# Batch norm's scale in the last stage: from ScalarE alone to GpSimd and ScalarE by turns

## The chip, the cores and the metric

The kernel runs on one core of a Trainium2 chip. The metric is the device time of one execution in microseconds. Before the change it is 2118.17 us, the median of six runs (2117.89 to 2119.62). The core has five engines that matter here: TensorE (PE) multiplies matrices, VectorE (DVE), ScalarE (ACT) and GpSimd (POOL) work elementwise, and SyncE (SP) issues DMA transfers. Each works through its own queue in order and waits on semaphores for the others.

## The reference

Sixteen images x of 128 channels and 32x32 pixels, in f32, pass through an attention layer and a residual block of two quantized convolutions. What matters here is the end of the second:

```python
out = act_quant(x)
out = conv3x3(out, weight_quant(w1))
out = batchnorm(out, gamma1, beta1)
out = act_quant(out)
out = conv3x3(out, weight_quant(w2))
out = batchnorm(out, gamma2, beta2)
return out + identity
```

`batchnorm` takes mean and variance of each channel over all sixteen images, so no image can be scaled before the last one's second convolution is done. With the statistics known it is `y * scale + bias` with one scale and one bias per channel; then the block's input (`identity`) is added.

## The kernel before

Channels lie on the 128 partitions, so an image is a tile of 128x1024 f32 (512 KB). `fast_path` runs in two parts. The first, the attention of all images and the first convolution, takes nearly all of the span; the attention's result of each image is stored to DRAM (`x1_dram`). The second part (lines 836 to 876) brings these back as `res0` to `res15` (`x1` in the code), computes the first batch norm's parameters, and then goes over the images: `quantize` the image, nine matmuls per piece in `conv` (L273), ScalarE's copy out of PSUM into the image's tile `ys[b]` (L284), VectorE's `bn_stats` (L283, L289). Between them `check_sums` (L337 to L351) works out a flag, with one `partition_all_reduce` on GpSimd (L350); if it is set, a slower general path runs afterwards (L1061, L1062), which is not the case with these inputs.

`bn_params(1)` (L306 to L327) then turns the statistics into `scale2` and `bias2`, in a chain of small VectorE instructions and one of ScalarE. It ends with the bias (L324). Everything before this point is left as it is.

The last stage is lines 866 to 876. It goes over the images in order; some of the first are cut into parts along their pixels. For each part there are three steps: `y * scale2 + bias2` in place, on VectorE for the first two parts of image 0 (L872) and on ScalarE for all else (L874); the addition of the residual in place, on VectorE (L875), with both inputs in SBUF; and the store to `out`, issued by SP (L876).

The order of instructions on each engine is set by the tile framework's scheduler, which takes the program's order with dependencies in mind; each engine then runs its own list in order. A tile's addition waits for its scaling and for its `res` transfer, a store waits for its addition.

GpSimd has sixteen instructions in the whole span: memsets at the start (L222, L231, L236, L296), the identity for transposes (masks.py, lines 197 and 199), two `partition_all_reduce` for the convolution weights (L1042) and the one of L350. [...]

Of the kernel before, what the change touches and what calls it, by code (L numbers as in the profile page):

```python
# [12 lines left out]
ALU = mybir.AluOpType  # L13
# [176 lines left out]
def fast_path(  # L190
# [13 lines left out]
    B, C, N = x.shape  # L204
# [27 lines left out]
    ys = [keep.tile([P, N], F32, name=f"y{b}") for b in range(B)]  # L232
# [6 lines left out]
    def quantize(b, src, scale, bias, r0=0, r1=H):  # L239

        cut = slice(r0 * W, r1 * W)
        t = qtp.tile([P, (r1 - r0) * W], F32, tag="qt", name="qt")
        if b == B - 1 and scale == A_LEVELS and r1 == H:
            nc.vector.tensor_scalar(t, src[:, cut], scale, 0.0, ALU.mult, ALU.max)
        else:
            nc.scalar.activation(t, src[:, cut], AF.Relu, bias=bias, scale=scale)
        nc.vector.tensor_scalar(t, t, A_LEVELS, MAGIC, ALU.min, ALU.add)
        return nc.vector.tensor_scalar(  # L248
            pads[b % NPAD][:, r0 + 1 : r1 + 1, 1 : W + 1],
            t.rearrange("p (h w) -> p h w", w=W),  # L250
            MAGIC,
            None,
            ALU.subtract,
        )
# [7 lines left out]
    def gather(n):  # L262
        nc.vector.bn_aggr(late[n][:, 1:3], early[n].rearrange("p g s -> p (g s)"))
        nc.vector.tensor_scalar(
            late[n][:, 2:3], late[n][:, 2:3], float((B - 1) * N), None, ALU.mult
        )

    def conv(pool, tag, b, n, r, rows=RPH, group=None, after=None):

        ps = pool.tile([P, rows, W], F32, tag=tag, name=f"psc{n}_{b}_{r}")  # L270
        for tap in range(NTAP):
            dy, dx = divmod(tap, 3)
            last = nc.tensor.matmul(  # L273
                ps,
                lhsT=wq[n][:, tap, :],
                rhs=pads[b % NPAD][:, r + dy : r + dy + rows, dx : dx + W],
                start=(tap == 0),
                stop=(tap == NTAP - 1),
            )
        ps = ps.rearrange("p h w -> p (h w)")  # L280
        if group is not None:
            with tc.issue_after(after) if after else nullcontext():
                nc.vector.bn_stats(place(n, b, group), ps)  # L283
        nc.scalar.copy(ys[b][:, r * W : (r + rows) * W], ps)  # L284
        return last

    def statistics(b, n):
        for hf in range(NHF):
            last = nc.vector.bn_stats(place(n, b, hf), ys[b][:, ts(hf, HALF)])  # L289
        return last  # L290
# [15 lines left out]
    def bn_params(n):  # L306

        new = lambda what: keep.tile([P, 1], F32, name=f"{what}{n}")
        mv = keep.tile([P, 2], F32, name=f"mv{n}")
        nc.vector.bn_aggr(mv, late[n])  # L310
        mean, var = mv[:, 0:1], mv[:, 1:2]
        rt = new("rt")
        nc.scalar.activation(rt, var, AF.Sqrt, bias=eps, scale=ss[:, n : n + 1])
        v = new("v")
        nc.vector.tensor_scalar(v, var, ss[:, n : n + 1], BN_EPS, ALU.mult, ALU.add)
        r = new("r")
        nc.vector.reciprocal(r, rt)

        t = new("t")
        nc.vector.tensor_scalar(t, r, r, v, ALU.mult, ALU.mult)  # L320
        nc.vector.tensor_scalar(t, t, -0.5, 1.5, ALU.mult, ALU.add)
        scale, bias = new("scale"), new("bias")
        nc.vector.tensor_scalar(scale, r, t, gs[:, n : n + 1], ALU.mult, ALU.mult)
        nc.vector.scalar_tensor_tensor(  # L324
            bias, mean, scale, be[:, n : n + 1], ALU.mult, ALU.subtract, reverse1=True
        )
        return scale, bias  # L327
# [9 lines left out]
    def check_sums():  # L337

        sums_range(B - 1)
        ok = keep.tile([P, 2], F32, name="ok")  # L340
        low, high = keep.tile([P, 1], F32, name="low"), keep.tile([P, 1], F32, name="high")
        nc.vector.tensor_reduce(low, ext[:, 0, :], AX.X, ALU.min)
        nc.vector.tensor_reduce(high, ext[:, 1, :], AX.X, ALU.max)
        nc.vector.tensor_scalar(ok[:, 0:1], low, 1.0 / SUM_LIMIT, None, ALU.is_ge)
        nc.vector.tensor_scalar(ok[:, 1:2], high, SUM_LIMIT, None, ALU.is_le)
        bad = keep.tile([P, 1], F32, name="bad")
        nc.vector.tensor_tensor(bad, ok[:, 0:1], ok[:, 1:2], ALU.mult)
        nc.vector.tensor_scalar(bad, bad, -1.0, 1.0, ALU.mult, ALU.add)
        worst = keep.tile([P, 1], F32, name="worst")
        nc.gpsimd.partition_all_reduce(worst, bad, P, bass_isa.ReduceOp.max)  # L350
        nc.vector.tensor_copy(flag, worst[0:1, :])  # L351

    with ExitStack() as ph:
# [454 lines left out]
        while step < n_steps or later:  # L808
            if step < n_steps:
                g, j = divmod(step, NCH)  # L810
                b, h = heads[g]
# [24 lines left out]
    with ExitStack() as ph:  # L836
        pool = lambda name, bufs, **kw: ph.enter_context(tc.tile_pool(name=name, bufs=bufs, **kw))
        resp = pool("res", 1)
        ps_c = pool("ps_c", 6, space=PSUM)
        scale1, bias1 = bn_params(0)  # L840
        x1 = []
        for b in range(B):
            t = resp.tile([P, N], F32, name=f"res{b}")
            nc.sync.dma_start(out=t, in_=x1d[b])
            x1.append(t)

        for r0, r1 in ((0, 10), (10, RPH + 2), (RPH + 2, H)):
            quantize(0, ys[0], scale1, bias1, r0, r1)
        quantize(1, ys[1], scale1, bias1)
        starts = {0: (0, 8, RPH, H), B - 1: (0, RPH, H - 8, H)}  # L850
        for b in range(B):
            rows = starts.get(b, (0, RPH, H))
            for i, (r0, r1) in enumerate(zip(rows, rows[1:])):
                conv(ps_c, "c", b, 1, r0, r1 - r0, group=i if b == B - 1 else None)
            if b + 2 < B:
                quantize(b + 2, ys[b + 2], scale1, bias1)
            if b < B - 1:
                done = statistics(b, 1)
            if b == B // 2:
                with tc.issue_after(done.ins):  # L860
                    check_sums()
            if b == B - 2:
                gather(1)
        scale2, bias2 = bn_params(1)

        parts = {0: (0, N // 4, N // 2, N), 1: (0, N // 2, N), 2: (0, N // 2, N)}
        for b in range(B):
            ends = parts.get(b, (0, N))
            for lo, hi in zip(ends, ends[1:]):
                y = ys[b][:, lo:hi]  # L870
                if b == 0 and hi <= N // 2:
                    nc.vector.tensor_scalar(y, y, scale2, bias2, ALU.mult, ALU.add)  # L872
                else:
                    nc.scalar.activation(y, y, AF.Identity, bias=bias2, scale=scale2)  # L874
                nc.vector.tensor_tensor(y, y, x1[b][:, lo:hi], ALU.add)  # L875
                nc.sync.dma_start(out=out[b][:, lo:hi], in_=y)  # L876
    outer.close()
# [107 lines left out]
def attention_then_quantized_convs(  # L985
# [48 lines left out]
    def conv_weights(n, wp, behind):  # L1034
# [19 lines left out]

    flag = const.tile([1, 1], mybir.dt.int32, name="flag")
    fast_path(
        nc, tc, x, wqk, wvo, bo, bnp, x1d, out, bo_sb, bnp_sb, quad, wq, sc, flag, conv_weights,
        constants,
# [81 lines left out]
```

## Time and profile before

| What | Value |
|---|---|
| median of six runs | 2118.17 us |
| the profiled execution, its own time | 2117.95 us |
| its span, from first to last instruction | 2116.1 us |
| PE busy | 2084.5 us (99%) |
| DVE busy | 1454.5 us (69%) |
| ACT busy | 735.9 us (35%) |
| POOL busy | 6.8 us, 16 instructions |
| last bias known (L324) | 2089.56 us |
| L874 on ACT, 128x1024, x13 | 1225 ns each |
| L874 on ACT, 128x512, x5 | 801 ns each |
| L872 on DVE, 128x256, x2 | 408 ns each |
| L875 on DVE, 128x1024, x13 | 1217 ns each |
| L875 on DVE, 128x512, x5 | 680 ns each |
| L875 on DVE, 128x256, x2 | 414 ns each |
| output stores, 512 KB, x13 | 4.1 us from issue to landing (median) |
| output stores, all 20 | 1.7 to 5.4 us from issue to landing |
| stores of `x1_dram`, 512 KB, x16 | 2.6 us from issue to landing (median) |

Times inside the execution are counted from the start of the span. The execution's own time is 1.85 us longer than its span. Consecutive instructions of one engine overlap a little: where VectorE's additions of 1217 ns stand back to back, they start every 1.13 us, those of 680 ns every 0.60 us, those of 256 elements every 0.33 us. The stage that the change touches is the time from 2089.6 us to the end.

### The profile page before, as it was taken

To read this page: it belongs to the slowest core of one execution; us is meant where nothing else is said; L and a number is where in the kernel's file an instruction comes from. 1 tells how busy PE (TensorE), PEld (TensorE's weight loads), DVE (VectorE), ACT (ScalarE), POOL (GpSimd) and SP (SyncE) were. 2 spreads that over 40 slices of the span, in tenths; PEclk is the share of its full clock that TensorE was granted. 3 is DMA by queue.
4 is the path that set the end of the run, shared out by engine and by line. 5 is a ranking of instruction groups with operands and counts; after the bars stand their busy time and mean duration, and the time that the engine had idled before them with its cause. 6 is when DMAs were issued, how large, how long until landed. Compare 5 with 4: busy or idle time off the path is not lost.

```text
span 2116.1 us, 14861 instructions
## 1 busy us (share of the span) xinstructions
PE 2084.5 (99%) x5276; PEld 941.0 (44%) x5277; DVE 1454.5 (69%) x2171; ACT 735.9 (35%) x858; POOL 6.8 (0%) x16
## 2 busy tenths in 40 slices
PE   9999999999999999999999999999999999999994
PEld 4444444444444444444444444444444444444542
DVE  4775677767577676667658666776757667676776
ACT  2333333333333333333333333333333333333365
POOL 0000000000000000000000000000000000000000
PEclk9999999999999999999999999999999999999997
DMA  2000000000000000000000000000000000000044
GB/s 61 12 20 0 0 20 0 20 0 10 11 0 20 0 20 0 1 20 0 20 1 20 0 0 20 0 20 0 13 8 0 20 0 10 0 0 10 1 170 160
DMA packets 11089, 36.81 MB, mean 17 GB/s; under 512 B 1536, under 2 KB 1920, under 8 KB 11008
## 3 DMA queue, kind: packets, MB, share of 16 engines
q1 hardware_dynamic: 9824, 33.10, 4.3%
q10 hardware_dynamic: 1184, 2.69, 0.4%
q8 instruction: 43, 0.70, 0.1%
q14 instruction: 38, 0.31, 0.0%
HBM read 19.01 MB, written 16.78 MB: 17 GB/s over the span
## 4 chain that ended last, share of the span: by engine, by line
PE 98%; DVE 1%; ACT 0%; DMA 0%; issue 0%; ACTq 0%; DVEq 0%
PE pss L487 42%; PE psa L511 41%; PE psv L466 5%; PE psu L453 5%; PE psc L273 3%; PE psw L720 1%; DVE y L875 1%; PE psa L628 1%; ACT y L874 0%; DMA x<-in_x_dram 0%; DVE es L620 0%; PE psr L552 0%; DVEq L1061 0%; DVE late L283 0%; PE ps_b L425 0%
## 5 line engine op out<-in xcount | busy, mean ns | idle before, releaser
L500 ACT ACTIVATE e<-pss 128x1024 f32<-128x1024 f32 x511 | 522.8, 1023 | 1280.4 <-PE pss L487 1244.2
L487 PE MATMUL pss<-u,x 128*128 128x512 f32 (+1 forms) x2064 | 962.4, 589 | 0.0
L511 PE MATMUL psa<-e,vo 128*128 128x512 f32 x2016 | 947.8, 592 | 0.0
L522 DVE TENSOR_TENSOR es<-es,e 128x1024 f32<-128x1024 f32 x378 | 460.5, 1218 | 291.4 <-ACT e L500 291.3
L487 PEld LDWEIGHTS pss<-u,x 128*128 128x128 f32 x2064 | 392.1, 190 | 487.2 <-issue 470.9
L511 PEld LDWEIGHTS psa<-e,vo 128*128 128x128 f32 x2016 | 378.1, 190 | 452.2 <-issue 451.0
L474 DVE COPY vo<-psv 128x512 f32<-128x512 f32 x128 | 88.2, 689 | 265.1 <-PE psv L466 265.1
L453 PE MATMUL psu<-x,at_sb 128*128 128x512 f32 x256 | 131.5, 595 | 0.8 <-DMA x<-in_x_dram 0.5
L466 PE MATMUL psv<-bt_sb,x 128*128 128x512 f32 x256 | 130.2, 592 | 0.0
L534 DVE TRANSPOSE_TENSOR_REDUCE part<-es 128x32 f32<-128x1024 f32 (+1 forms) x66 | 80.6, 1221 | 2.2
L520 DVE TENSOR_TENSOR es<-e,e 128x1024 f32<-128x1024 f32 x63 | 76.6, 1216 | 6.3 <-ACT e L500 6.3
L570 DVE STREAM_TRANSPOSE rb<-sums 128x1024 f32<-128x1024 f32 (+1 forms) x66 | 79.8, 1209 | 1.3
L453 PEld LDWEIGHTS psu<-x,at_sb 128*128 128x128 f32 x256 | 48.7, 191 | 62.3 <-issue 60.3
L466 PEld LDWEIGHTS psv<-bt_sb,x 128*128 128x128 f32 x256 | 48.6, 190 | 61.2 <-issue 57.6
L711 DVE TENSOR_TENSOR tiles<-rows 128x1024 bf16<-128x1024 bf16 x60 | 71.8, 1218 | 1.1 <-PE psw L720 0.6
L458 DVE TENSOR_SCALAR u<-psu,au_sb 128x512 f32<-128x512 f32 x64 | 47.6, 744 | 34.5 <-PE psu L453 34.5
L273 PE MATMUL psc<-pad,wq 128*128 128x512 bf16 (+3 forms) x333 | 67.8, 365 | 0.6 <-DVE pad L248 0.6
L727 ACT COPY wino<-psw 128x512 f32<-128x512 f32 x120 | 64.2, 593 | 0.0
L581 DVE TENSOR_TENSOR av<-av,rb 128x1024 f32<-128x1024 f32 x47 | 57.3, 1220 | 0.4
L582 DVE TENSOR_TENSOR acc<-acc,av 128x1024 f32<-128x1024 f32 x47 | 57.1, 1215 | 0.0
L273 PEld LDWEIGHTS <-wq 128*128 128x128 bf16 x333 | 32.2, 97 | 36.4 <-PE unread L755 1.1
L527 ACT COPY av<-psa 128x512 f32<-128x512 f32 x63 | 36.9, 585 | 29.8 <-PE psa L511 29.8
(121 smaller groups left out, 746.9 us busy)
## 6 DMA issues: line engine op xcount, KB each, us to landing
x_dram<-x SPq DMA_DIRECT2D x16, 512.0 KB, 2.6
res<-x_dram SPq DMA_DIRECT2D x16, 512.0 KB, 9.4
x<-in_x_dram SPq DMA_DIRECT2D x14, 512.0 KB, 3.6
out_dram<-y SPq DMA_DIRECT2D x13, 512.0 KB, 4.1
out_dram<-y SPq DMA_DIRECT2D x5, 256.0 KB, 2.3
raw<-in_cw_dram ACTq DMA_DIRECT2D x2, 576.0 KB, 3.7
x<-in_x_dram ACTq DMA_DIRECT2D x1, 512.0 KB, 3.7
wqk_sb<-in_wqk_dram ACTq DMA_DIRECT2D x1, 385.5 KB, 4.2
```

The source lines that it names most:

```text
L273: last = nc.tensor.matmul(ps, lhsT=wq[n][:, tap, :], rhs=pads[b % NPAD][:, r + dy : r + dy + rows, dx : dx + W], start=(tap == 0), stop=(t ...
L453: nc.tensor.matmul(ps, lhsT=at_sb[:, h, :], rhs=xt[b][:, ts(hf, HALF)], start=True, stop=True)
L466: nc.tensor.matmul(ps, lhsT=xt[b][:, ts(j, P)], rhs=bt_sb.rearrange("p h o -> p (h o)"), start=True, stop=True,)
L474: nc.vector.tensor_copy(vos[b, j], ps)
L487: last = nc.tensor.matmul(ps[:, ts(m, N // len(parts))], lhsT=xt[b][:, ts(key, P)], rhs=us[g][:, queries], start=True, stop=True,)
L500: exps[:] = [nc.scalar.activation(e, ps, AF.Exp).ins]
L511: nc.tensor.matmul(psa[g][m], lhsT=vos[b, j][:, ts(h, P)], rhs=e[:, ts(m, HALF)], start=(j == 0), stop=(j == NCH - 1),)
L520: nc.vector.tensor_tensor(es[g], es.pop((g, 0)), es.pop((g, 1)), ALU.add)
L522: added = nc.vector.tensor_tensor(es[g], es[g], es.pop((g, j)), ALU.add)
L534: nc.vector.tensor_reduce(part, total.rearrange("p (k c) -> p k c", c=Q), AX.X, ALU.add, apply_transpose=True,)
L570: nc.vector.transpose(rb, rinv.unsqueeze(2).to_broadcast([P, n, Q]))
L711: nc.vector.tensor_tensor(tiles[b][:, l % 2], pick(x), pick(y), op)
```

## The change

The parts of the first images are cut otherwise, and the scaling is given out by the image's number. Image 0 keeps its three parts (256, 256 and 512 pixels), of which VectorE scales the first, and ScalarE the other two. Image 1 is still stored in two halves, but GpSimd scales it whole, in one instruction, before its first half. Image 2 is no longer cut. From there on ScalarE scales the even images and GpSimd the odd ones, each whole. VectorE does all additions, as before, and SP issues all stores.

```diff
-        parts = {0: (0, N // 4, N // 2, N), 1: (0, N // 2, N), 2: (0, N // 2, N)}
+
+        parts = {0: (0, N // 4, N // 2, N), 1: (0, N // 2, N)}
         for b in range(B):
             ends = parts.get(b, (0, N))
-            for lo, hi in zip(ends, ends[1:]):
+            for i, (lo, hi) in enumerate(zip(ends, ends[1:])):
                 y = ys[b][:, lo:hi]
-                if b == 0 and hi <= N // 2:
+                if (b, i) == (0, 0):
                     nc.vector.tensor_scalar(y, y, scale2, bias2, ALU.mult, ALU.add)
-                else:
+                elif b % 2 == 0:
                     nc.scalar.activation(y, y, AF.Identity, bias=bias2, scale=scale2)
+                elif i == 0:
+                    nc.gpsimd.tensor_scalar(ys[b], ys[b], scale2, bias2, ALU.mult, ALU.add)
                 nc.vector.tensor_tensor(y, y, x1[b][:, lo:hi], ALU.add)
                 nc.sync.dma_start(out=out[b][:, lo:hi], in_=y)
```

The line numbers move by up to three: in the changed kernel VectorE's scaling is L873, ScalarE's scaling is L875, GpSimd's L877, the addition L878, the store L879. In the instruction lists of the changed kernel, ScalarE has 9 scalings for 18, VectorE one for two and 19 additions for 20, GpSimd eight, with a change of its code ahead of the first, and SP 19 stores for 20. On VectorE and SP the first half of image 1 now stands ahead of the last half of image 0. TensorE's list is the same.

## The prediction

> **What bounds the kernel now.** The page's first part puts TensorE at 99% of the span, and the 40 slices show it busy up to the last: only that last slice, of 53 us, is not full. The change lies behind the last matmul, so I read that end alone, in this order: the chain that ended last, the stage second by second, then GpSimd's own list.
>
> The chain of waits, from the end of the second batch norm's parameters on:
>
> ```profile
> 2089.34 0.23 DVE bias L324
> 2089.57 0.03 issue
> 2089.59 5.90 ACT y L874 x7
> ...
> 2096.68 6.79 DVE y L875 x6
> ...
> 2106.88 1.23 DVE y L875
> 2108.11 1.02 DVEq L1061
> 2109.13 0.10 DVE y L875
> ```
>
> Here ScalarE's scaling sets the pace first (5.90 us for seven pieces), then VectorE's additions, 6.79/6 = 1.13 us from start to start. The last addition ends at 2109.23. But the span ends at 2116.1, so the transfers decide. The busy time second by second (the last two columns are the share of the DMA engines and GB/s):
>
> ```profile
> 2090.00:2091.00 1.00, 0.00 (x0) 0.00 (x0) 1.00 (x5) 1.00 (x2) 0.00 (x0) 1.00 0.00 0
> 2091.00:2092.00 1.00, 0.00 (x0) 0.00 (x0) 1.00 (x2) 1.00 (x3) 0.00 (x0) 0.84 0.38 130
> ...
> 2096.00:2097.00 1.00, 0.00 (x0) 0.00 (x0) 1.00 (x2) 1.00 (x2) 0.00 (x0) 0.50 0.57 231
> 2097.00:2098.00 1.00, 0.00 (x0) 0.00 (x0) 1.00 (x2) 1.00 (x2) 0.00 (x0) 0.50 1.00 406
> ...
> 2112.00:2113.00 1.00, 0.00 (x0) 0.00 (x0) 0.00 (x0) 0.00 (x0) 0.00 (x0) 0.50 1.04 410
> 2113.00:2114.00 1.00, 0.00 (x0) 0.00 (x0) 0.00 (x0) 0.00 (x0) 0.00 (x0) 0.50 0.34 131
> ```
>
> The reader is to see that the DMA engines are full (about 400 GB/s) from 2097 to 2113, while VectorE (third pair of columns) has stopped at 2109. At 400 GB/s an image of 524 KB takes 1.31 us, and VectorE delivers one in 1.13: **the output transfer is the bound of this stage**, and a backlog of about 4 us stands when VectorE is done. Loss there is only the start, up to 2092, and the hole at 2096 (0.43 us idle), where the first whole image came late. So a pair of images may take VectorE up to 2 x 1.31 = 2.62 us before the transfers run dry; now it takes 2.26, which leaves 0.36 us.
>
> **The change, part by part.** ScalarE: 18 instructions become 9. From the rows of L874, a 1024-wide one takes 1225 ns, started every 1.13 us, a 512-wide one 801 ns; the 256-wide one is not in the trace, I put it on the line through both, 0.59 us (bounds 0.37, the line at nothing, and 0.80). In all about 9 us of work in place of 18.34. ScalarE is off the path. VectorE: one `tensor_scalar` of 256 goes (0.33 us from start to start), the additions stay; y2's two of 512 (2 x 0.60) become one of 1024 (1.13). Its own work is then 0.33 + 2 x 0.33 + 3 x 0.60 + 14 x 1.13 + 0.09 (the last one's duration, 1.22, over its pitch) = 18.70 us; from 2089.59 it would end at 2108.29, 0.94 us before now. SP: 19 issues for 20, of 0.33 to 0.71 us, below an image's 1.13 either way; nothing is behind them. The order on VectorE changes as well: image 1's first half now stands ahead of image 0's last half, and waits for GpSimd's whole image 1; image 0's last half, scaled by about 2090.9, queues behind that wait. TensorE, and all that comes before the stage, keep their instructions and order.
>
> GpSimd: nothing before, now eight `tensor_scalar` of 128x1024 f32, and one instruction ahead of them without a tile (a change of its code; it has no wait and stands right behind L350, which ends at 2063.24). The first such change is in the trace: 7.61 us of issue ahead of the identity's select. Here 26 us of convolutions cover it, so I cost it at nothing; without that cover the stage would be 7.6 us later. The second change, ahead of the first `partition_all_reduce`, cost nothing at the first use: that one started at 55.46, 0.14 us after VectorE's result (53.97 + 1.35). [...]
>
> What does one 128x1024 `tensor_scalar` cost on GpSimd? No row has it. The nearest, from GpSimd's list:
>
> ```profile
> L222 POOL MEMSET sums<- 128x256 f32 x1 | 0.3, 311 | 0.3 <-POOLq L1124 0.3
> masks.py:199 POOL TENSOR_SCALAR_AFFINE_SELECT ident<-ident 128x128 f32<-128x128 f32 x1 | 0.3, 282 | 7.6 <-issue 7.6
> masks.py:197 POOL MEMSET ident<- 128x128 f32 x1 | 0.2, 204 | 0.0
> ```
>
> The memsets give (311 - 204)/128 = 0.84 ns an element and 97 ns fixed: 0.95 us for 1024, the low bound, as they neither read nor compute. The select reads, computes and writes, as ours does: with the memsets' fixed part it is (282 - 97)/128 = 1.45 ns an element, 1.58 us, the high bound; with the memsets' slope it is 175 ns fixed and 1.03 us. I take 1.2 us, between the two readings of the select, the row that it is nearest to. [...]
>
> Does it lie beside VectorE's additions? If it did, eight times 1.2 us would be free, since a pair has 2.26 us. Three rows speak to that: the same `partition_all_reduce` of 128x1, under an addition of two SBUF tensors and without one:
>
> ```profile
> 86.83 1.22 DVE L582 TENSOR_TENSOR acc<-acc,av 128x1024 f32<-128x1024 f32 x1
> 87.02 1.24 POOL L1042 PARTITION_ALL_REDUCE alpha<-pmax  x1 [30.32 <-DVE pmax L1040]
> ...
> 2062.89 0.35 POOL L350 PARTITION_ALL_REDUCE worst<-bad  x1 [1974.63 <-DVE bad L348]
> ```
>
> Alone it takes 0.35 us; started 0.19 us into the addition it ends at 88.26, 0.21 us after the addition's end (88.05). The one at 55.46 does the same: its addition ends at 56.46, it at 56.70. So GpSimd, reading SBUF, **waited for VectorE's addition to finish**; the addition kept its 1.22 us. [...]
>
> Nearly all that VectorE does in this stage is such additions, back to back. GpSimd gets its turn when VectorE waits, and VectorE waits for it at every odd image. So the two add up. Each odd image costs 1.2 us and the 0.09 us by which two additions no longer overlap: 8 x 1.29 = 10.3 us. VectorE ends at 2108.29 + 10.3 = 2118.6, 9.4 us later than now. A pair now takes 2.26 + 1.29 = 3.55 us, over the 2.62 of its transfers, so these run dry and no backlog stands at the end. The tail is 0.03 us to the issue, 2.6 us (median issue to landing of the x_dram stores of the same 512 KB, which go out singly) and 1.4 us from the last landing to the span's end (the last issue at 2109.26 and the longest landing, 5.4, make 2114.7). Now that tail is 6.9 us, then 4.0. End: 2118.6 + 4.0 = 2122.6, 6.5 us over 2116.1. The profiled execution took 2117.95, its span and 1.85 around it; with 6.5 it is 2124.5. The median of the runs lies 0.22 above it: **2124.7 us**.
>
> With 0.95 us an image the sum is 2.0 lower, 2122.7. With 1.58 and a hand-over of 0.24 (the 0.21 to 0.24 between the addition's end and GpSimd's) it is 8 x (1.82 - 1.20) = 5.0 higher, 2129.7.
>
> **Rivals.**
> 1. GpSimd runs ahead: if it gets the port after each addition rather than when VectorE stops, all eight are done early and VectorE does the last images at 1.13 us against 1.31. Some eight to eleven of them leave 1.4 to 2 us of backlog: about 2126.4. The trace has no case of two waiting at once.
> 2. Not slower: GpSimd's `tensor_scalar` runs beside the additions (the waits above might belong to `partition_all_reduce` alone, another code). It decides at 0.36 us: as long as an odd image costs VectorE less, the transfers hide it. Then VectorE's first wait for image 1 is some 0.3 us, the first issue comes 0.33 us earlier, and of the hole at 2096 up to 0.43 us may close; I take 0.6 us: 2117.6.
> 3. They share element by element: 16 images of 1.07 us (1024 elements at the slope of the additions, (1.13 - 0.60)/512 a unit) and 8 of 0.86 (memset's slope) make 24 us; from 2089.9 VectorE ends at about 2114, and with the 4.0 us of tail at 2118: 2 us slower, 2120.
> 4. GpSimd is slower than any row suggests, 1.8 to 2.1 us with its hand-over: 2130 to 2132.
> 5. The code change is not hidden: 2124.7 + 7.6 = 2132.3.
>
> **How the numbers follow.** Forecast 0.42 (with its bounds 2122.7 to 2129.7), rival 1 0.22, rival 2 0.12, rival 3 0.12, rival 4 0.08, rival 5 0.04. The range from 2119.5 to 2132.0 leaves out rivals 2 and 5, 0.16. About 0.2% (4.2 us) is what a measurement here can tell from no change: slower is over 2122.4. Forecast and rivals 1, 4 and 5 are slower, 0.76; rivals 2 and 3 are within, 0.24, of which I give 0.01 to faster.
>
> **What would show it.** In the profile after: VectorE's last addition near 2118 to 2119 and no longer on ScalarE; idle time of L878 put down to GpSimd's `y`, or additions stretched to 2 us; GpSimd's instructions long while an addition runs; holes in the transfers in every pair of images, and the last landing under 4 us from its issue. Wrong if the additions keep their 1.13 us pitch through odd images (rival 2), or if GpSimd's first start is far behind 2089.6 (rival 5).

## The result, and the profile after

The changed kernel takes **2123.21 us** (median of 19 runs), the kernel before 2118.06 in the same sessions (39 runs): a ratio of 1.0024, 95% interval 1.0018 to 1.003. It is 5.15 us slower; forecast was 6.5 us, and the range held it.

The profiled execution has a span of 2121.5 us, 5.4 more. The end of the last parameter (L324) lies at 2089.56 before and 2089.79 after; from there to the span's end it was 26.51 us and is now 31.68. I call this the **stage**, and use it below for all kernels, since the executions differ by up to 2.6 us in when the first matmul of the attention (L487) starts (6.8 to 9.5 us), which has nothing to do with the stage. One profile of each kernel is on record.

The chain of waits of the changed kernel:

```profile
2089.57 0.23 DVE bias L324
...
2090.00 0.73 POOL y L877
...
2091.30 23.68 POOL y L877 x7
2114.99 0.02 issue
2115.01 1.22 DVE y L878
```

Where ScalarE and VectorE stood, GpSimd stands now, from 2090 to 2115. The stage's instructions by shape (count, busy us and mean ns, idle before them and its releaser):

```profile
L877 POOL TENSOR_SCALAR y<-y,scale,bias 128x1024 f32<-128x1024 f32 x8 | 25.0, 3133 | 26.5 <-DVE bias L324 26.5
L878 DVE TENSOR_TENSOR y<-y,res 128x1024 f32<-128x1024 f32 x14 | 18.0, 1337 | 3.7 <-POOL y L877 3.7
```

GpSimd's instruction has a mean of 3.13 us, and VectorE's additions 1337 ns in place of 1217: they are stretched, and on top of that VectorE waited 3.7 us. From the timeline, a late pair (first fence) and an early addition (second):

```profile
2108.37 3.31 POOL L877 TENSOR_SCALAR y<-y,scale,bias 128x1024 f32<-128x1024 f32 x1
2108.41 1.23 DVE L878 TENSOR_TENSOR y<-y,res 128x1024 f32<-128x1024 f32 x1 [0.94 <-POOL y L877]
2109.56 1.22 DVE L878 TENSOR_TENSOR y<-y,res 128x1024 f32<-128x1024 f32 x1
```

```profile
2093.40 3.19 POOL L877 TENSOR_SCALAR y<-y,scale,bias 128x1024 f32<-128x1024 f32 x1
...
2095.61 2.05 DVE L878 TENSOR_TENSOR y<-y,res 128x1024 f32<-128x1024 f32 x1
```

In the first, neither addition is stretched (1.23 and 1.22 us); GpSimd's instruction ends at 2111.68, 0.90 us after the second addition (2110.78), and VectorE waits for its result. In the second it is VectorE that is held: GpSimd ends at 2096.59, the addition 1.07 us later, at 2097.66. So each shuts the other out. The transfers, second by second (the last two columns are the share of the DMA engines and GB/s):

```profile
2106.00:2107.00 1.00, 0.00 (x0) 0.00 (x0) 1.00 (x2) 0.00 (x0) 1.00 (x1) 0.50 0.65 258
...
2113.00:2114.00 1.00, 0.00 (x0) 0.00 (x0) 1.00 (x1) 0.00 (x0) 1.00 (x1) 0.50 0.27 107
...
2115.00:2116.00 1.00, 0.00 (x0) 0.00 (x0) 0.99 (x1) 0.00 (x0) 0.00 (x0) 0.50 0.99 401
```

They now run dry in every pair of images (0.65, 0.27), where before they were full from 2097 to 2113 (a share of 0.99 to 1.05 in each second).

### The profile page after: what moved, and what is told of

Its sections match the earlier page's. It is cut to its first block, busy times and chain, and to the rows that moved or that the text cites. A ratio compares the mean times of both kernels' runs of the same rounds, so it can differ in the third digit from the quotient of the medians.

```text
span 2121.5 us, 14859 instructions
## 1 busy us (share of the span) xinstructions
PE 2084.0 (98%) x5276; PEld 941.1 (44%) x5277; DVE 1457.8 (69%) x2169; ACT 726.8 (34%) x849; POOL 31.8 (2%) x24
## 4 chain that ended last, share of the span: by engine, by line
PE 98%; POOL 1%; DVE 0%; DMA 0%; ACT 0%; issue 0%; ACTq 0%; POOLq 0%
PE pss L487 41%; PE psa L511 41%; PE psv L466 5%; PE psu L453 5%; PE psc L273 3%; PE psw L720 1%; POOL y L877 1%; PE psa L628 1%; DMA x<-in_x_dram 0%; DVE es L620 0%; DVE y L878 0%; PE psr L552 0%; DVE late L283 0%; PE ps_b L425 0%; ACTq L387 0%
## 5 line engine op out<-in xcount | busy, mean ns | idle before, releaser
L487 PE MATMUL pss<-u,x 128*128 128x512 f32 (+1 forms) x2064 | 962.4, 589 | 0.0
L487 PEld LDWEIGHTS pss<-u,x 128*128 128x128 f32 x2064 | 392.1, 190 | 487.2 <-issue 471.2
L520 DVE TENSOR_TENSOR es<-e,e 128x1024 f32<-128x1024 f32 x63 | 76.6, 1216 | 7.0 <-ACT e L500 7.0
```

The costliest lines, as they stand in the source:

```text
L487: last = nc.tensor.matmul(ps[:, ts(m, N // len(parts))], lhsT=xt[b][:, ts(key, P)], rhs=us[g][:, queries], start=True, stop=True,)
L520: nc.vector.tensor_tensor(es[g], es.pop((g, 0)), es.pop((g, 1)), ALU.add)
```

## The experiments

Theory: a GpSimd instruction that reads SBUF and a VectorE addition with two SBUF inputs exclude each other, so GpSimd's work is added to VectorE's. What only one of the two can hold I call the port, as the prediction does, and a stretch in which GpSimd holds it its turn; the word stands for the exclusion as it was measured, not for a part of the chip that a trace shows. Rivals: GpSimd is slow by itself and VectorE only waits for it; the new first parts and orders cost the time. All edits are against the changed kernel. The kernel before, run beside them, had medians of 2117.7 to 2118.0 us.

| Kernel | Stage, us | Median, us | Ratio to before, interval |
|---|---|---|---|
| before | 26.51 | 2118.06 | |
| changed | 31.68 | 2123.21 | 1.0024, 1.0018 to 1.003 |
| e1 second input from PSUM | 26.81 | 2119.48 | 1.0004, 0.9995 to 1.0013 |
| e2 ScalarE takes the odd images | 26.99 | 2117.86 | 1.0, 0.9991 to 1.0009 |
| e3 VectorE takes the odd images | 29.62 | 2121.54 | 1.0016, 1.0007 to 1.0025 |
| e4 GpSimd only writes | 27.30 | 2118.40 | 1.0003, 0.9994 to 1.0012 |
| e5 four images on GpSimd | 29.12 | 2120.37 | 1.0011, 1.0002 to 1.002 |
| e6 GpSimd's work doubled | 39.60 | 2130.42 (one run) | |
| e7 even images first | 30.88 | 2123.06 (one run) | |
| e8 images 1 and 3 | 28.25 | 2119.77 | 1.0011, 1.0002 to 1.002 |
| e9 images 11 and 13, late | 28.72 | 2120.40 | 1.0011, 1.0002 to 1.002 |
| e10 the same, in order | 28.54 | 2120.17 | 1.001, 1.0001 to 1.0019 |
| e11 image 11, late | 27.09 | 2118.52 | 1.0003, 0.9994 to 1.0012 |
| e12 image 1, at once | 27.12 | 2118.31 | 1.0001, 0.9992 to 1.001 |

**e1: one input from PSUM.**

```diff
+        zero = pool("ps_z", 1, space=PSUM).tile([P, N], F32, name="zero")
...
+            if b == 4:
+                nc.vector.memset(zero, 0.0)
...
-                nc.vector.tensor_tensor(y, y, x1[b][:, lo:hi], ALU.add)
+                nc.vector.tensor_tensor(y, y, zero[:, lo:hi], ALU.add)
```

> The changed kernel, but each addition takes its second input from a zeroed PSUM tile in place of the residual in SBUF, so the residual is left out of the output. Theory (one port: GpSimd's read of SBUF and an addition with two SBUF inputs exclude each other): GpSimd's eight instructions fall from 3.3 to 4.3 us to 0.9 to 1.1 us each, VectorE keeps its pitch of 1.13 to 1.2 us through odd images with no wait for GpSimd after the first, and the transfers bound the stage again: 2117.2 to 2118.5 us. Rival (GpSimd's own speed is the price, whatever VectorE does): its instructions stay above 3 us and VectorE still waits for them, 2122 to 2124 us.

By shape:

```profile
L881 DVE TENSOR_TENSOR y<-y,zero 128x1024 f32<-128x1024 f32 x14 | 15.9, 1210 | 0.0
L880 POOL TENSOR_SCALAR y<-y,scale,bias 128x1024 f32<-128x1024 f32 x8 | 9.5, 1204 | 26.5 <-DVE bias L324 26.5
```

The same eight instructions of GpSimd now take 1.20 us beside additions of 1.21, and VectorE waits for none of them (0.0). So GpSimd's own speed is not the price: 1.9 of its 3.1 us in the changed kernel were waiting. The median is 1 us over what I expected, but the stage (26.81) is not: the added memset of the PSUM tile delays the convolutions ahead of it by 0.75 us (60 matmuls from their first start took 14.30 us, 13.55 before).

**e2: the new parts alone.**

```diff
-                elif b % 2 == 0:
+                else:
                     nc.scalar.activation(y, y, AF.Identity, bias=bias2, scale=scale2)
-                elif i == 0:
-                    nc.gpsimd.tensor_scalar(ys[b], ys[b], scale2, bias2, ALU.mult, ALU.add)
```

> The new first parts alone: ScalarE scales all odd images too, GpSimd none. Theory (the loss is GpSimd's): ScalarE's pitch of 1.13 us is just enough, VectorE ends near 2109.3 in the span and the time is within 0.5 us of the kernel before, 2117.7 to 2118.6 us. Rival (the uncut image 2 and the order of image 1 ahead of image 0's last part cost the time): 2120 to 2123 us.

As the theory said: the parts and orders cost 0.48 us of stage and nothing that the times show.

**e3: VectorE does it itself.**

```diff
-                    nc.gpsimd.tensor_scalar(ys[b], ys[b], scale2, bias2, ALU.mult, ALU.add)
+                    nc.vector.tensor_scalar(ys[b], ys[b], scale2, bias2, ALU.mult, ALU.add)
```

> VectorE scales the odd images itself, in place of GpSimd. Theory (a GpSimd image takes 1.03 us out of VectorE's time: 0.90 of holding the port and the hand-over): VectorE's own tensor_scalar of 128x1024 takes 0.69 us and some 0.60 from start to start, so a pair is 2.86 us in place of 3.29; VectorE ends near 2113 and the time is 2119.2 to 2120.5 us, some 3 us below the changed kernel. Rival (taking work off VectorE helps, and something else loses the time): giving it back costs 8 x 0.6 = 4.8 us, 2127 to 2129 us.

The instruction takes 802 ns and adds 0.73 us to a pair, not 0.60, so the median lies 1 us above my expectation. The order is as expected: with all scaling of odd images back on VectorE the stage is 2.06 us shorter than with GpSimd's help. GpSimd's help costs VectorE more than the work.

**e4: GpSimd writes, but reads nothing.**

```diff
-                    nc.gpsimd.tensor_scalar(ys[b], ys[b], scale2, bias2, ALU.mult, ALU.add)
+                    nc.scalar.activation(ys[b][:, 0:1], ys[b][:, 0:1], AF.Identity, bias=bias2, scale=scale2)
+                    nc.gpsimd.memset(ys[b], 1.0)
```

> GpSimd writes the odd images without reading SBUF: a memset of 128x1024 in place of its tensor_scalar (odd images are not scaled; a one-column scaling on ScalarE ahead of each memset keeps it behind the parameters). Theory (what excludes is the shared read: an addition with two SBUF inputs against a GpSimd instruction that reads): the memsets take about 0.95 us each beside the additions, VectorE keeps 1.13 us an image, the time is 2117.5 to 2118.7 us. Rival (any GpSimd access to SBUF shuts VectorE out, or the odd images' waits for GpSimd alone cost the time): VectorE is stretched or waits as with the changed kernel, 2122 to 2124 us.

```profile
L879 DVE TENSOR_TENSOR y<-y,res 128x1024 f32<-128x1024 f32 x14 | 16.0, 1216 | 0.0
...
L878 POOL MEMSET y<- 128x1024 f32 x8 | 7.6, 951 | 31.2 <-ACT y L877 30.7 <-ACTq L1066 0.5
```

Additions with both inputs in SBUF, and GpSimd's writes of the same 512 KB beside them: neither is stretched (1216 and 951 ns). So GpSimd's write excludes nothing here. That leaves its read or its arithmetic, since a memset has neither, and no run takes these two apart. On VectorE's side it is the second SBUF input: in e1 the arithmetic stayed on both engines, that input went, and the exclusion with it (1.21 and 1.20 us). The two timelines above show the blocking in both directions (3.31 us for GpSimd's instruction, 2.05 us for the addition). Which of the two started first does not settle it alone: in the late pair GpSimd's instruction starts at 2108.37, 0.04 us before the first addition and 1.19 before the second, and both additions go ahead of it; in the early one it starts 2.21 us before the addition, and the addition is held.

**e6: the cost doubled.**

```diff
+        spare = resp.tile([P, N], F32, name="spare")
...
                     nc.gpsimd.tensor_scalar(ys[b], ys[b], scale2, bias2, ALU.mult, ALU.add)
+                    nc.gpsimd.tensor_scalar(spare, x1[b], scale2, bias2, ALU.mult, ALU.add)
```

> The changed kernel with the suspected cost doubled: behind each scaling GpSimd scales the residual of the same image into a spare tile that nobody reads, so no new wait comes in. Theory (each GpSimd instruction takes 0.9 to 1.03 us of VectorE's time): 8 x 0.9 to 1.03 more, the stage is 38.5 to 40 us in place of 31.68 and the time about 2130 to 2132 us. Rival (GpSimd's instructions hide where VectorE is not waiting for them): the stage grows by less than 4 us, 2127 us or less.

39.60 - 31.68 = 7.92 us for eight more: 0.99 each, as expected. The first eight cost the stage only 4.69 us over e2 (0.59 each), since the transfers hid part of them; with the transfers dry, a further one costs its full price. Most of it shows as waiting: VectorE's idle time for GpSimd's `y` rises from 3.7 to 9.6 us, the busy time of its 14 whole additions from 18.0 to 20.4.

**e7: who gets the port.**

```diff
-        for b in range(B):
+        for b in [*range(0, B, 2), *range(1, B, 2)]:
```

> The loop takes all even images first, then the odd ones, so that VectorE's list has seven additions in a row that wait for no GpSimd result. In the changed kernel a GpSimd instruction that waited got its turn after three additions. Theory A (a turn after three additions, whatever they wait for): GpSimd finishes one image for every three additions in that stretch, four or five of its eight before the first of the odd images after image 1 is added. Theory B (GpSimd gets in only where VectorE has nothing ready): it finishes image 1 and then nothing until VectorE waits for image 3, some 8 us later, and that instruction is over 7 us long. The time is 2121.5 to 2124 us by either, since the shares of the port add up the same.

Theory A. GpSimd had finished images 1, 3, 5 and 7 when VectorE began image 3's addition at 2104.71, and image 9 a microsecond later. One of its instructions, and the addition that its turn before had held up:

```profile
2100.46 2.05 DVE L878 TENSOR_TENSOR y<-y,res 128x1024 f32<-128x1024 f32 x1
2101.43 4.26 POOL L877 TENSOR_SCALAR y<-y,scale,bias 128x1024 f32<-128x1024 f32 x1
```

4.26 us is the rest of the addition that GpSimd's last turn had held (1.08 us), two additions of 1.14 and its own 0.90: here its turn comes after three additions, the held one counted (the last section says where that fails). In the changed kernel images 7 and 9 take 4.26 us as well; the three before them took 1.30, 2.12 and 3.19. So rival 1's idea, GpSimd running ahead, holds for the first half of the stage; later VectorE waits for every odd image.

**e5: half the images.**

```diff
-                elif b % 2 == 0:
+                elif b % 4 != 1:
```

> GpSimd scales only images 1, 5, 9 and 13, ScalarE all others after image 0. Theory (1.03 us of VectorE's time an image, of which the transfers hide what fits under their 1.31 us an image): four images take 4 x 1.13 + 1.03 = 5.55 us against 5.24 of transfers, VectorE ends near 2112, the time is 2118.2 to 2119.5 us: more than half of the loss goes. Rival (each GpSimd image costs the end the same): half of 5.15 us stays, 2120.3 to 2121 us.

The theory's number was wrong: 2.13 us over e2 remain, near the rival's half. GpSimd did not spread its four turns over the stage as I had reckoned; it ran ahead, and all four were over by 2102.18, in the first 11 us of the stage. My idea was that no backlog of transfers had grown by then that could hide them. e8 to e12 test that.

**e8: two early** (`elif b not in (1, 3)` goes to ScalarE).

> GpSimd scales images 1 and 3 only, free to start at once; ScalarE all others after image 0. With four images the loss was 2.4 us, not the 0.3 to 1 expected; the idea now is that GpSimd ran ahead, so its turns fell into the first 12 us, where no backlog of transfers stands that could hide them. Theory (early turns are lost whole, less what VectorE would have waited for ScalarE): the stage from the last parameter to the end is 0.7 to 1.5 us longer than with ScalarE alone (26.99 us), 2118.6 to 2119.4 us. Rival (any two turns hide under 18 images' slack): within 0.4 us of ScalarE alone.

1.26 us over e2: as expected. The median, 2119.77, lies 0.4 above what I expected.

**e9: two late.**

```diff
-                elif b % 2 == 0:
+                elif b not in (11, 13):
...
-                    nc.gpsimd.tensor_scalar(ys[b], ys[b], scale2, bias2, ALU.mult, ALU.add)
+                    gate = keep.tile([P, 1], F32, name=f"gate{b}")
+                    nc.vector.tensor_scalar(gate, ys[b - 4][:, 0:1], 0.0, scale2, ALU.mult, ALU.add)
+                    nc.gpsimd.tensor_scalar(ys[b], ys[b], gate, bias2, ALU.mult, ALU.add)
```

> GpSimd scales images 11 and 13 only, and each starts behind the addition four images before (its scale is made by a one-column VectorE instruction from that image's sum, times zero). Theory: by then the transfers are 1.5 to 2 us behind VectorE, the two turns of 1.03 us hide, and the stage is within 0.4 us of ScalarE alone (26.99 us), 2117.7 to 2118.4 us. Rival (each turn costs the end its 0.6 to 0.65 us wherever it lies, as four cost 2.4 and eight 5.2): 1.2 us longer, 2119 us or more.

1.73 us over e2: the theory missed, and it is more than the rival's 1.2. But the transfers do not show the rival's picture (three stretches, the last two columns as above):

```profile
2104.00:2107.00 3.00, 0.00 (x0) 0.00 (x0) 2.22 (x2) 1.67 (x2) 0.75 (x1) 0.50 1.01 401
2107.00:2109.00 2.00, 0.00 (x0) 0.00 (x0) 1.40 (x3) 0.00 (x0) 1.56 (x1) 0.50 1.01 412
2109.00:2112.00 3.00, 0.00 (x0) 0.00 (x0) 2.36 (x2) 0.00 (x0) 0.47 (x1) 0.50 0.35 138
```

They stay full through the first turn (2104) and past it; the hole comes with the second. There image 14 was added first, but its store stood behind image 13's in SP's list.

**e10: the same with VectorE held to the images' order.**

```diff
+        prev = None
...
-                nc.vector.tensor_tensor(y, y, x1[b][:, lo:hi], ALU.add)
+                with tc.issue_after(prev) if prev else nullcontext():
+                    prev = nc.vector.tensor_tensor(y, y, x1[b][:, lo:hi], ALU.add).ins
```

> As e9_two_late, with VectorE's additions held in the order of the images. In e9 the first late turn left the transfers full, and the hole of 1.8 us came at 2109: image 14 had been added ahead of image 13, but its store stood behind image 13's in SP's list. Theory (a turn hides where a backlog of transfers stands): the stage from the last parameter to the end is 26.9 to 27.5 us, within 0.5 of ScalarE alone (26.99 us), and the transfers are full from 2097 to the end; 2117.7 to 2118.6 us. Rival (each turn costs the end 0.6 us or more wherever it lies): 28.2 us or more, 2119 us or more.

It failed again: 28.54. Image 11 once more left the transfers full; the hole came at 2111, after image 13 (full to 2111, then a share of 0.41 up to 2113). With the order held, image 13's one-column instruction stood right ahead of its addition, so VectorE lay idle for GpSimd's whole instruction, 1.40 us. And the backlog that I had set against the turns, 2 us, is that of the stage's end; at 0.18 us an image it is 1.6 at image 11 by my estimate, and what is left of it at image 13 is less than the second turn.

**e11: image 11 alone** (`elif b != 11`, else as e9).

> GpSimd scales image 11 only, behind VectorE's addition of image 7. In the two runs with images 11 and 13 the transfers stayed full through the turn for image 11, and the hole came at image 13: together VectorE lost 2.8 us, and the backlog at image 13 was not the 2 us I had counted for the end of the stage but what was left of some 1.6 us. Theory (a turn hides where a backlog of transfers stands): with one turn there is no hole after 2097, the stage is 26.8 to 27.3 us (ScalarE alone 26.99), 2117.6 to 2118.4 us. Rival (each turn costs the end 0.6 to 0.8 us wherever it lies): 27.6 to 27.8 us, 2118.5 us or more.

0.10 us over e2, and no hole behind 2098; GpSimd's instruction ran from 2104.09 to 2107.22:

```profile
2104.00:2107.00 3.00, 0.00 (x0) 0.00 (x0) 2.15 (x2) 3.00 (x4) 2.91 (x1) 0.50 1.01 401
2107.00:2110.00 3.00, 0.00 (x0) 0.00 (x0) 2.75 (x3) 2.27 (x3) 0.22 (x1) 0.50 1.03 410
2110.00:2115.00 5.00, 0.00 (x0) 0.00 (x0) 3.02 (x3) 0.00 (x0) 0.00 (x0) 0.50 1.02 403
```

In the stage, one late turn hides. The median, 2118.52, is at the rival's bound; the interval of the ratio, 0.9994 to 1.0012, is some 4 us wide and decides nothing here.

**e12: image 1 alone** (`elif b != 1`).

> GpSimd scales image 1 only, at once, as in the changed kernel. Theory (an early turn has no backlog to hide in; images 1 and 3 together cost 1.26 us): VectorE's first addition takes 1.3 us in place of 0.41, the first store goes out some 0.9 us later, and the stage is 27.4 to 27.9 us, 0.4 to 0.9 over ScalarE alone. Rival (a single turn is too small to matter, early or late): 26.8 to 27.3 us.

This one missed: 0.13 us over e2, the rival's size. The first store does go out late, but e2 has a hole of its own, where VectorE waits for ScalarE; the same second in e2 (first fence) and in e12:

```profile
2094.00:2095.00 1.00, 0.00 (x0) 0.00 (x0) 1.00 (x2) 1.00 (x2) 0.00 (x0) 0.50 0.30 117
```

```profile
2094.00:2095.00 1.00, 0.00 (x0) 0.00 (x0) 1.00 (x2) 1.00 (x2) 0.00 (x0) 0.50 0.98 377
```

Freed of image 1, ScalarE has image 2 ready at 2091.80 in place of 2093.14. VectorE starts image 2's addition at the same moment in both (2093.18, and 2093.17 in e2): e2 waits for ScalarE up to there, e12 does not. So the one turn is paid with that wait, and the hole closes. The next (e8) has nothing left to be paid with.

By the stage alone early and late do not differ: one turn costs 0.10 or 0.13 us, two cost 1.26 early and 1.55 to 1.73 late. That a late turn is hidden by the backlog and an early one by a wait is read from the transfers and from the times of the additions, one profile each.

No variant beat the kernel before: its transfers are full from 2097 on, and behind the start a hole of 0.43 us is left to gain.

## Why the prediction was right

- **What bounds the stage**: right. It is the transfers: in e11 VectorE ends 1.32 us later than in e2 (21.22 us after the parameters, 19.90 in e2), and the stage grows by 0.10.
- **GpSimd's duration**, 1.2 us from the two readings of the select's row: right, 1.19 us where nothing excludes it (e1; the first one 1.30). The part that shuts VectorE out is shorter, 0.90 (2110.78 to 2111.68 in the late pair). The change of code is the instruction MODIFY_POOL_CONFIG; the traces show its place and its time, not what it does. In the trace before it stands at 4.3, in the 7.61 us of idle time ahead of the select. Here it stands at 2063.4, 26 us before GpSimd's first instruction, and that started at 2090.00, 0.21 us after the parameters: no such stretch showed. What it would cost without those 26 us no run shows.
- **The two add up**: right, and shown: e1 and e4 take the exclusion away, one from each side, and the loss goes (stages of 26.81 and 27.30 us against 31.68); e6 adds to it (39.60). How they add was right only in part: four of the eight turns came where VectorE waited, as the sum had it, the first four where an addition was held.
- **The size, 8 x 1.29 us**: this is the term that was too large. A pair takes 3.30 us (from 2105.07 to 2108.37), 1.04 over 2.26, not 1.29. Of GpSimd's 1.19 us (e1) only 0.90 came behind the addition that it waited for; by that difference, the other 0.29 lay beside it. A turn that held an addition cost still less, 0.84 to 0.89 (2.05 us for 1.21). VectorE's last addition ended 26.44 us after the parameters; the sum had 29.0.
- **The tail**: this term was too small. It is 5.2 us from VectorE's end, forecast 4.0; the last store took 3.7 us to land, not 2.6. The stores of the pairs before it took 2.6 to 2.9; why the last took longer the runs do not show. The two errors have opposite signs, and that 6.5 came so near to 5.2 is luck.
- **Rivals**: GpSimd running ahead (1) happened in part, and without the backlog that I gave it: it ended with image 7, and the pairs after it take VectorE 3.30 us against 2.62 of transfers. Running side by side (2), sharing by elements (3) and a late code change (5) did not happen: additions stop for whole instructions (the one at 2095.61 took 2.05 us for 1.21 and ended 1.07 after GpSimd's), and the code change (MODIFY_POOL_CONFIG) stands at 2063.4 in the trace.

## What to carry to other kernels

Before work goes to GpSimd, look at what VectorE does meanwhile: here, beside additions of two SBUF tensors, GpSimd's scaling of a 128x1024 f32 image in SBUF was not parallel work but a loan of VectorE's time, 0.84 to 1.04 us an image, more than VectorE needed to do it (0.73). In this stage, bound by transfers, such a loan was free, as e9 to e11 read, only as far as the backlog at that moment reached (0.10 us for one late turn, 1.55 to 1.73 for two), so reckon the backlog image by image, not at the end. And measure a change at the end of a long kernel by the stage's own length, since whole times scatter by 2 us and more. The engines' part of it repeats to 0.01 us (image 2's addition starts 3.91 to 3.92 us after the parameters in e2, e9, e10 and e11); how well the transfers repeat is not shown.

## What the runs showed that was not expected

GpSimd's wait for its turn beside back-to-back additions was the same, within 0.01 us, in the three executions read for it. Its first five instructions took 1.30, 2.12, 3.19, 4.26 and 4.26 us in the changed kernel; e7's were 1.31, 2.12, 3.20, 4.26 and 4.26 with a sixth of 4.26, and e5's four were 1.31, 2.12, 3.19 and 4.26. The first finds none ahead of it (it takes 1.30 in e1 too). From the second on, three additions go ahead each time, the one that was held counted, and the times grow because these additions grow: the rest of a 256-wide one, a 256-wide and a 512-wide one (1.21 us), then the rest of a 512-wide one, one of 512 and one of 1024 (2.29), then three of 1024 (3.35), each time with 0.90 of its own on top.

Three is no fixed number, though. In e6 one addition (2104.60 to 2105.84) goes ahead and the next, which is ready, is held:

```profile
2104.55 2.28 POOL L879 TENSOR_SCALAR spare<-res,scale,bias 128x1024 f32<-128x1024 f32 x1
...
2105.77 2.13 DVE L880 TENSOR_TENSOR y<-y,res 128x1024 f32<-128x1024 f32 x1
```

Why three, and why one there, the runs do not say.
